# A reordered layer norm, more scan steps beside the first one, more buffers and doubled costs, in a two-layer image kernel

## The chip, the core and the metric

The kernel runs on one core of a Trainium2 chip. The core has five engines with instruction queues of their own: PE (TensorE, matrix products into PSUM), DVE (VectorE, elementwise work and scans), ACT (ScalarE, activation functions with a scale and a bias), POOL (GpSimd, elementwise work on SBUF) and SP (SyncE, which here only issues transfers). ACT and POOL issue transfers too. [...]PEld is the loading of weights into PE.

The metric is device time in microseconds (us) of one launch, the median of several runs.

## The reference

The input x is four images of 96 channels and 128 x 128 pixels, float32. Two residual layers follow each other, and only their skeleton matters here:

```python
# layer 0: a selective scan over the pixels in four orders
z  = silu(depthwise3x3(in_w @ groupnorm(x) + in_b))           # 192 channels
for k in range(4):                  # rows, columns, and both reversed
    delta, B, C = softplus(...), ..., ...                     # from z, per pixel
    h[t]  = exp(delta * A) * h[t-1] + delta * B * z[t]        # the scan
    ym   += C * h + D * z
yn = (ym - mean(ym)) * rsqrt(var(ym) + 1e-5)                  # over the 192 channels
x  = x + out_w @ (yn * ln_w + ln_b) + out_b                   # "the norm" below

# layer 1, on groupnorm(x)
xr, x1, x2 = relu_split_norm(groupnorm(x))    # positive and negative half, each normed
key, qry, value = conv3x3(x1), conv3x3(x2), conv3x3(x1)       # "the maps"
w  = softmax(unfold(key) @ unfold(qry).T)                     # 96 x 96 x 3 x 3 weights
y1 = layernorm(conv3x3(value, w))                             # "attention"
y2 = layernorm(conv3x3(x2, w_conv2)) * x1
x  = x + xr + w_full @ [y1, y2] + b_full
```

## The kernel before

The whole kernel is one launch. It is written as Python generators, one for each stage of each image. A generator emits a few instructions and then yields a number, its own estimate of what they cost. `co_run(left, right, pace)` runs two generators together: whenever `left` yields a cost, `right` is advanced until it has yielded `pace` times as much. So the numbers in the `yield` statements decide which instructions of two stages become neighbours in the engines' queues. `chain` puts generators one behind another, and `drain` runs one to its end.

The stages, in the order of the program:

1. `project` makes layer 0's inputs from each image; beside it runs `ssm_scan`, the scan over all four images. The scan advances in steps of 1024 pixels of 128 channels, each step in two half-steps that yield 2.6 each. A half-step issues three matrix products on PE (two of `pBC`, one of `pd`, line 736), and on DVE a product, the scan and a product (lines 826, 843, 847). A step has two operations on POOL (lines 822 and 855), and a softplus in two halves and an exponential on ACT (lines 665 and 798).
2. `norm` of image 0, then `split` of image 0, beside the scan at pace 0.5. `norm` is `ssm_output`, `split` is `split_norm`.
3. `direct_maps` of image 0, three convolutions done tap by tap (line 2102), beside the rest of the scan at pace 1.15; when the scan has ended, beside `norm` and then `split` of image 1 at pace 1.0. Only behind the scan, `lifting` is set: the value map is then read back, four rows at a time, turned into planes (`pixel_planes`, lines 1428 to 1437, on DVE) and stored for the last convolution. After each set of six rows up to four such lifts are made, and the rest at the end, by `lift(H)`.
4. `attend` of images 0 to 3, the `left` generator of the rest of the kernel. For image 0 only the last convolution remains (`direct_maps` made its maps). For the others it makes the maps in transformed planes (`products`, `outputs`, lines 1471 to 1564), the softmax, and the last convolution. Beside image b's attention runs what is called `light`: `norm` and `split` of image b+1 and `close` of image b-1 (`attn_output`, which makes the output rows of an image). Beside the last image there are no further `norm` and `split`; `light` is `close` of image 2 and then two passes of `LastOutput`: `before`, which prepares the last image's own x1 and residual, and `beside`, which can only start when the last image's maps are done.

The order in which the instructions were emitted is pinned, engine by engine, from the first projections to the end of the scan (`in_order(first)`). Behind that point a scheduler orders each engine's instructions, starting from the order of emission.

`ssm_output` works on 16 tiles of 1024 pixels in 18 passes of its loop; each pass handles three tiles: `new` (squares and sums), `mid` (variance, root, reciprocal) and `old` (output). For a `new` tile, ACT squares the 192 channels in two parts (`squares`, into the buffer `sq`, of which there is one), PE sums values and squares over the channels (`sums`, line 950), ACT copies the sums out and its queue sends them to 8 partitions (`rows`: `st`, `mq`). For `mid`, DVE makes the variance (`inverse`, lines 969 to 971), ACT its root (`roots`, line 975), DVE the reciprocal, and POOL's queue stores it to DRAM (`back`, line 988); `spread_out` reads it back, broadcast to 96 partitions, as `r` (line 996, POOL's queue), and `xr`, a tile of x from SP's queue, gets a bias on ACT. For `old`, PE projects the tile (`projected`, line 1002), DVE multiplies with `r` (line 1015, for image 0 line 1019), POOL adds `xr` (line 1016, for image 0 line 1020), DVE takes statistics (line 1021), and SP's queue stores the tile. In one pass these operations come in this order, with six yields between them:

```
projected(old, 0) | squares(new, 0) inverse(mid) roots(mid) scaled(old, 0) projected(old, 1) back(mid)
| sums(new, 0) squares(new, 1) bias and spread_out(mid) | scaled(old, 1) load_y sums(new, 1) | store(old) | rows(new) |
```

where `scaled` is the multiply, the add and the statistics in one.

`split_norm` reads the normed image twice. Its first pass only counts and sums (lines 1110 to 1117); its second pass makes the two halves x1 and x2. For image 0 each half of a tile is a buffer `half0` or `half1` (two of each) that POOL clears at its left edge, ACT scales, DVE thresholds (line 1230) and ACT's queue stores. For the other images the second pass also makes planes.

## Time and profile before

| | us |
|---|---|
| runs, median of 3 | 6656.29 |
| runs, lowest and highest | 6639.72, 6660.51 |
| profiled execution, its own time | 6633.8 |
| profiled execution, span of its instructions | 6631.9 |
| granted PE clock, mean over the span | 0.886 of full |

The profile belongs to one execution. Its own time lies below the lowest of the three runs, so a sum made from its durations is made against 6633.8 and then moved to the median. Durations, waits and stretches of time below are counted from the start of the span. A wait is listed as who waited, for whom, how long in total, how often, and the longest one. The stages begin as follows in it: the scan at 330, norm 0 at 2103, its split at 2384, the direct maps at 2545, the scan's end at 3290, image 0's last convolution at 3721, the maps of image 1 at 3867, of image 2 at 4730, of image 3 at 5775, and the last output at 6591.

### The profile page before, as it was taken

The numbers are of one execution on the slowest core, as the hardware profiler recorded it, in microseconds if no ns is written. First come the engines' busy times: TensorE is split into PE (matmuls) and PEld (weight loads), VectorE is DVE, ScalarE is ACT, GpSimd is POOL, SyncE is SP. The second block draws the span as 40 slices with busy tenths as digits, with TensorE's granted clock in tenths as the row PEclk, the third lists the DMA queues.
The fourth block names the chain that finished last, engine by engine and source line by source line (L and its number), as shares of the span: only waits on it lengthen the run. The fifth ranks groups of instructions, "written<-read, shape, count | busy, mean of one in ns | idle before, by whom it ended". The sixth has DMA issues, their size and how long they took to land. (4 is left out here: it accounts for less than half of the span.)

```text
span 6631.9 us, 76453 instructions
## 1 busy us (share of the span) xinstructions
PE 5374.8 (81%) x23264; PEld 2337.9 (35%) x23264; DVE 4907.7 (74%) x7469; ACT 3803.6 (57%) x4751; POOL 3506.9 (53%) x2744
## 2 busy tenths in 40 slices
PE   5889988987887736989987479877888777887988
PEld 2333323322222102444433134444333444344553
DVE  3247778988997568989755885588875788898666
ACT  1257768777786566676534464475544654545542
POOL 2236758978787436969621354466234574034320
PEclk9999989998997757999998789987988887998989
DMA  7766777866765667665666765655775555866547
GB/s 165 174 155 181 201 206 198 223 192 163 222 182 162 187 171 213 198 199 170 203 184 177 195 182 156 174 143 157 206 202 155 147 154 154 227 173 188 150 122 213
DMA packets 888487, 1198.29 MB, mean 181 GB/s; under 512 B 216143, under 2 KB 741015, under 8 KB 875597
## 3 DMA queue, kind: packets, MB, share of 16 engines
q1 hardware_dynamic: 864460, 1138.46, 63.1%
q0 software_dynamic: 16208, 38.42, 2.2%
q10 hardware_dynamic: 7408, 16.53, 0.8%
q8 instruction: 187, 3.06, 0.2%
q14 instruction: 224, 1.83, 0.1%
HBM read 777.62 MB, written 345.58 MB: 169 GB/s over the span
## 5 line engine op out<-in xcount | busy, mean ns | idle before, releaser
L622 PE MATMUL bank<-y,wp 128*128 128x512 f32 (+3 forms) x3584 | 1316.6, 624 | 85.5 <-DMA y<-y 34.4
L855 POOL TENSOR_TENSOR y<-y,dl 128x1024 f32<-128x1024 f32 x384 | 1056.4, 2751 | 272.1 <-DVE dl L847 238.0
L822 POOL TENSOR_TENSOR dl<-dl,u 128x1024 f32<-128x1024 f32 x384 | 1009.2, 2628 | 223.6 <-ACT dA L798 107.5
L843 DVE TENSOR_TENSOR_SCAN dA<-dA,pBC 128x512 f32<-128x512 f32 x768 | 981.5, 1278 | 30.7
L1471 PE MATMUL two<-ya,wd 128*64 128x192 f32 (+3 forms) x2376 | 595.1, 427 | 193.5 <-ACT odd L1542 96.8
L847 DVE TENSOR_TENSOR dl<-dA,pBC 128x512 f32<-128x512 f32 x768 | 528.0, 688 | 271.4 <-PE pBC L736 198.5
L736 PE MATMUL pBC<-xr,wbc 60*128 60x512 bf16 (+1 forms) x1536 | 458.8, 403 | 330.0 <-DVE dA L843 257.7
L622 PEld LDWEIGHTS bank<-y,wp 128*128 128x128 f32 (+3 forms) x3584 | 458.8, 169 | 754.2 <-issue 655.5
L2102 PE MATMUL bank<-y,wn 128*128 128x384 f32 (+5 forms) x2408 | 676.8, 504 | 43.0 <-DMA y<-x2d 18.9
L1905 ACT COPY yb<-ya 64x768 f32<-64x768 f32 (+1 forms) x660 | 537.8, 815 | 152.0 <-PE two L1471 111.7
L665 ACT ACTIVATE dl<-pd,dtb 128x512 f32<-128x512 f32 x768 | 485.6, 684 | 181.2 <-PE pd L736 171.3
L1471 PE MATMUL two<-yb,wd 128*64 128x192 f32 (+3 forms) x2376 | 567.6, 411 | 21.3 <-ACT yb L1905 21.3
L826 DVE TENSOR_TENSOR pBC<-dl,pBC 128x512 f32<-128x512 f32 x768 | 527.5, 687 | 9.7 <-POOL dl L822 8.8
L2102 PEld LDWEIGHTS bank<-y,wn 128*128 128x128 f32 (+3 forms) x2408 | 307.5, 167 | 338.9 <-issue 165.4
L798 ACT ACTIVATE dA<-dl,negA 128x1024 f32<-128x1024 f32 x384 | 420.3, 1141 | 2.3
L1471 PEld LDWEIGHTS two<-ya,wd 128*64 128x64 f32 (+1 forms) x2376 | 268.9, 172 | 405.4 <-ACT odd L1542 104.0
L736 PEld LDWEIGHTS <-wbc 60*128 60x128 bf16 (+1 forms) x1536 | 103.4, 96 | 767.7 <-issue 754.0
L665 ACT ACT_TABLE_LOAD x245 | 314.3, 1283 | 100.9 <-PE pd L736 93.6
L1975 POOL COPY own<-ring 32x512 f32<-32x512 f32 (+1 forms) x198 | 225.3, 1172 | 260.7 <-DVE ring L1564 224.4
L1471 PEld LDWEIGHTS two<-yb,wd 128*64 128x64 f32 (+1 forms) x2376 | 294.0, 173 | 167.5 <-issue 37.3
L2209 POOL MEMSET o<- 1x1024 f32 x60 | 56.3, 946 | 560.3 <-PE bank L2264 225.3
L1471 PE MATMUL two<-ya,wa 128*96 128x384 f32 (+1 forms) x528 | 230.1, 519 | 123.3 <-DMA ya<-vp 82.5
(323 smaller groups left out, 9936.6 us busy)
## 6 DMA issues: line engine op xcount, KB each, us to landing
u<-zb SPq DMA_DIRECT2D x192, 1024.0 KB
yms<-y SPq DMA_DIRECT2D x96, 512.0 KB
y<-yms SPq DMA_DIRECT2D x64, 768.0 KB
xn<-xnew SPq DMA_DIRECT2D x128, 384.0 KB
ya<-vp SPq DMA_DIRECT2D x120, 336.0 KB
y<-y SPq DMA_DIRECT2D x128, 258.2 KB
zb<-z SPq DMA_DIRECT2D x64, 512.0 KB
ya<-x1p SPq DMA_DIRECT2D x90, 336.0 KB
```

The lines of the kernel that those rows point to most:

```text
L622: nc.tensor.matmul(blocks(pz[p:e]), lhsT=ws[k][:, d, c : c + e - p], rhs=window(ys[k], at, d, n), start=(i == 0), stop=(i == len(terms) - 1),)
L665: nc.scalar.activation(dst, src, AF.Softplus, bias=bias)
L736: nc.tensor.matmul(p, lhsT=w[rows], rhs=xr[rows, at : at + CH], start=True, stop=True)
L798: nc.scalar.activation(live[m]["dA"], live[m]["dl"], AF.Exp, scale=negA[:, g % 3, k : k + 1])
L822: nc.gpsimd.tensor_mul(t, t, u_view(n))
L826: nc.vector.tensor_mul(p, live[n]["dl"][:, bass.ts(half, CH)], p)
L843: nc.vector.tensor_tensor_scan(h, h, p, init, ALU.mult, ALU.add)
L847: nc.vector.tensor_mul(live[n]["dl"][:, sl], live[n]["dA"][:, sl], live[n]["C", half])
L855: nc.gpsimd.tensor_add(v, v, t.rearrange("p (a b) -> p a b", b=W))
L1471: nc.tensor.matmul(of(to[p:e], r), lhsT=w[:, i, c : c + e - p], rhs=tiles(t[k][PAIR[i]][:, SLOT[i]], o, r), start=(k == 0), stop=False,)
L1905: nc.scalar.copy(yb[k][64 * h - 64 : 64 * h, :, :n], ya[k][0:64, :, h * TN : h * TN + n])
L2102: nc.tensor.matmul(pc[p:e, :n].rearrange("p (h w) -> p h w", w=W), lhsT=w[:, c : c + e - p], rhs=v[:, :, 0:W], start=(i == 0), stop=(i == ...
```

## The change

The change has four parts.

In `ssm_output`, `scaled` is taken apart into `scaled` (the multiply), `added` (the add) and `counted` (the statistics), and the operations of a pass are put in another order. `sq` gets two buffers, and the bank of PSUM for the sums is taken when the first sum is issued. With six yields of the same sizes as before, the pass becomes:

```
projected(old, 0) inverse(mid) squares(new, 0) | roots(mid) scaled(old, 0) projected(old, 1) squares(new, 1)
| back(mid) added(old, 0) scaled(old, 1) sums(new, 0) | sums(new, 1) added(old, 1) counted(old, 0) load_y
| rows(new) bias and spread_out(mid) counted(old, 1) | store(old) |
```

The pace of the scan beside norm 0 and split 0 goes from 0.5 to 0.65. The buffers `half0` and `half1` of image 0's split go from two to four each. And the costs yielded by `close` of image 2 and by `LastOutput.before` are doubled, so that they are spread over twice as much of the last image's attention.

The same operations are issued with the same shapes; nothing is added to or taken from the computation. The same line numbers hold up to line 940; behind it lines move by 3 to 17 (the sums are line 953 in the changed kernel, the multiplies 1015 and 1017, the statistics 1029).

```diff
--- before.py
+++ after.py
@@ -939,12 +939,15 @@
                     nc.sync.dma_start(ys[c], ym[:, :, bass.ts(c, SN)])
 
             def squares(c, j):
-                sq = p2.tile([C, SN], F32, name="sq", bufs=1)
+                sq = p2.tile([C, SN], F32, name="sq")
                 nc.scalar.activation(sq, ys[c][:, j], AF.Square)
-                sums_of[c] = sq, sums_of[c][1] if j else bank(ps)
+                sums_of[c, j] = sq
 
             def sums(c, j):
-                sq, pm = sums_of[c]
+                sq = sums_of.pop((c, j))
+                if j == 0:
+                    sums_of[c] = bank(ps)
+                pm = sums_of[c]
                 for g in range(4):
                     rhs = sq if g % 2 else ys[c][:, j]
                     nc.tensor.matmul(
@@ -954,12 +957,9 @@
                         start=(j == 0),
                         stop=(j == 1),
                     )
-                if j == 0:
-                    squares(c, 1)
-
             def rows(c):
                 st = p2.tile([128, CH], F32, name="st", bufs=1)
-                nc.scalar.copy(st, sums_of.pop(c)[1])
+                nc.scalar.copy(st, sums_of.pop(c))
                 mq = made[c] = p2.tile([RS, 2, W], F32, name="mq")
                 for i in range(2):
                     nc.scalar.dma_start(mq[:, i], st[32 * i : 32 * i + 65 : 64])
@@ -1009,16 +1009,24 @@
                 return po
 
             def scaled(c, h, po):
+                r = near[c][1][:, bass.ts(h, CH)]
+                if turned:
+                    v = r.rearrange("p (h j t) -> p h j t", t=TN, j=TW)
+                    nc.vector.tensor_mul(v, turned_view(po), v)
+                else:
+                    nc.vector.tensor_mul(r, po, r)
+
+            def added(c, h):
                 xr, r = (t[:, bass.ts(h, CH)] for t in near[c])
                 if turned:
                     v = r.rearrange("p (h j t) -> p h j t", t=TN, j=TW)
-                    nc.vector.tensor_mul(v, turned_view(po), v)
                     nc.gpsimd.tensor_add(v, v, turned_view(xr))
-                    xr = r
                 else:
-                    nc.vector.tensor_mul(r, po, r)
                     nc.gpsimd.tensor_add(xr, r, xr)
-                nc.vector.bn_stats(stats[:, 2 * c + h], xr)
+
+            def counted(c, h):
+                t = near[c][turned]
+                nc.vector.bn_stats(stats[:, 2 * c + h], t[:, bass.ts(h, CH)])
 
             for c in range(3):
                 load_y(c)
@@ -1028,37 +1036,46 @@
                 mid = c - 1 if 1 <= c <= NS else None
                 if old is not None:
                     po = projected(old, 0)
-                yield 1.2
+                if mid is not None:
+                    inverse(mid)
                 if new:
                     squares(c, 0)
+                yield 1.2
                 if mid is not None:
-                    inverse(mid)
                     roots(mid)
                 if old is not None:
                     scaled(old, 0, po)
                     po = projected(old, 1)
                     ys.pop(old)
+                if new:
+                    squares(c, 1)
+                yield 1.4
                 if mid is not None:
                     back(mid)
+                if old is not None:
+                    added(old, 0)
+                    scaled(old, 1, po)
+                if new:
+                    sums(c, 0)
                 yield 1.4
                 if new:
-                    sums(c, 0)
+                    sums(c, 1)
+                if old is not None:
+                    added(old, 1)
+                    counted(old, 0)
+                    load_y(c + 1)
+                yield 1.4
+                if new:
+                    rows(c)
                 if mid is not None:
                     xr = near[mid][0]
                     nc.scalar.activation(xr, xr, AF.Identity, bias=outbs)
                     spread_out(mid)
-                yield 1.4
                 if old is not None:
-                    scaled(old, 1, po)
-                    load_y(c + 1)
-                if new:
-                    sums(c, 1)
+                    counted(old, 1)
                 yield 1.4
                 if old is not None:
                     nc.sync.dma_start(xnew[:, bass.ts(old, SN)], near.pop(old)[turned])
-                yield 1.4
-                if new:
-                    rows(c)
                 yield 1.4
 
     def split_norm(xnew, x1d, x2d, stats, keep, cnt, ps, side, planes, vector, done):
@@ -1215,7 +1232,7 @@
                         )
                         k, parts = TW * R, 2
                     else:
-                        h = p2.tile([C, RS * PW], F32, name=f"half{side_}")
+                        h = p2.tile([C, RS * PW], F32, name=f"half{side_}", bufs=4)
                         hv = h.rearrange("p (h w) -> p h w", w=PW)
                         nc.gpsimd.memset(hv[:, :, 0:1], 0.0)
                         v, to = y.rearrange("p (h w) -> p h w", w=W), hv[:, :, 1:PW]
@@ -2227,7 +2244,7 @@
     def plain(v):
         return v.rearrange("p (h t j) -> p h t j", j=TW, t=TN)
 
-    def attn_output(img, ps, side):
+    def attn_output(img, ps, side, share):
         ob = out[img.b].rearrange("c h w -> c (h w)")
         with (
             tc.tile_pool(name="f1", bufs=1, side=side) as p1,
@@ -2267,7 +2284,7 @@
                         nc.vector.tensor_add(x1[:, sl], pf, e[:, sl])
                     else:
                         nc.vector.tensor_add(plain(x1[:, sl]), pixels(pf), pixels(e[:, sl]))
-                    yield 2.6
+                    yield 2.6 * share
                 nc.sync.dma_start(ob[:, bass.ts(t, SN)], x1)
 
     class LastOutput:
@@ -2303,9 +2320,9 @@
                         ahead = load(t + 1)
                     x1, e = (p3.tile([C, SN], F32, name=n) for n in ("x1", "e"))
                     first_half(img, xx, x1)
-                    yield 2.0
+                    yield 4.0
                     residual(img, xx, e)
-                    yield 2.6
+                    yield 5.2
                     for d, y in ((self.x1d, x1), (self.ed, e)):
                         nc.sync.dma_start(d[:, bass.ts(t, SN)], y)
 
@@ -2418,10 +2435,10 @@
         def attend(self, at):
             yield from attention(self, at)
 
-        def close(self, ps, side):
+        def close(self, ps, side, share=1.0):
             while not self.finished:
                 at.later.tick()
-            yield from attn_output(self, ps, side)
+            yield from attn_output(self, ps, side, share)
 
     npair = NB // 2
     zb, yms = (
@@ -2482,7 +2499,7 @@
     imgs = {0: Image(0)}
     imgs[0].begin()
     left = chain(imgs[0].norm(yms[0][0], psl, "left"), imgs[0].split(psl, "left"))
-    co_run(left, last, 0.5)
+    co_run(left, last, 0.65)
     drain(left)
     left = direct_maps(imgs[0], psl)
     co_run(left, last, 1.15)
@@ -2536,7 +2553,7 @@
                 after.append(
                     imgs[b + 1].split(psr, "right", lambda i, second: second)
                 )
-            after.append(imgs[b - 1].close(psr, "right"))
+            after.append(imgs[b - 1].close(psr, "right", 1.0 if b + 1 < NB else 2.0))
             if b + 1 == NB:
                 last = imgs[b].last = LastOutput(imgs[b], psr, "right")
                 imgs[b].maps_made = lambda: maps_made(last)
```

## The prediction

> **What bounds the kernel now.** I read the page first, then busy time by stretch, cut where the program changes stage, then the waits inside each stretch. The page says that no engine is full over the whole span:
>
> ```profile
> PE 5374.8 (81%) x23264; PEld 2337.9 (35%) x23264; DVE 4907.7 (74%) x7469; ACT 3803.6 (57%) x4751; POOL 3506.9 (53%) x2744
> ```
>
> So the stages have to be priced one by one. In the answer by stretch the columns are the stretch, its length, then busy us of PE, PEld, DVE, ACT, POOL, the granted PE clock, the DMA share and GB/s:
>
> ```profile
> 2103.00:2384.00 281.00, 188.02 (x476) 44.02 (x475) 146.81 (x223) 146.63 (x162) 130.18 (x96) 0.67 0.65 183
> 2384.00:2545.00 161.00, 30.62 (x61) 7.34 (x62) 125.04 (x172) 120.04 (x147) 41.18 (x47) 0.50 0.67 196
> 2545.00:3290.00 745.00, 686.76 (x2911) 319.25 (x2910) 644.78 (x784) 506.75 (x639) 630.27 (x239) 0.97 0.67 194
> 3290.00:3639.00 349.00, 286.77 (x1100) 122.97 (x1098) 175.43 (x473) 132.36 (x207) 72.63 (x135) 0.91 0.68 181
> 3639.00:3721.00 82.00, 0.25 (x2) 0.00 (x0) 81.66 (x224) 19.25 (x26) 31.71 (x62) 0.50 0.61 162
> 3721.00:3950.00 229.00, 182.59 (x775) 85.78 (x776) 199.15 (x332) 150.70 (x198) 107.64 (x134) 0.91 0.76 206
> 5810.00:6150.00 340.00, 273.46 (x1408) 141.98 (x1408) 295.67 (x377) 162.91 (x186) 135.33 (x137) 0.89 0.65 181
> 6150.00:6400.00 250.00, 231.74 (x1734) 155.30 (x1734) 151.72 (x294) 127.54 (x172) 111.70 (x166) 0.97 0.48 126
> ```
>
> In order: norm 0 beside the scan; split 0 beside the scan; image 0's direct maps beside the scan; the same beside norm 1; a gap of 82 us in which PE does nothing while VectorE is full; image 0's last convolution; and two halves of the last image's maps. Norm 0 has nothing full: it is a chain of waits. The waits in 2103 to 2384 us (total, times, longest) show its links:
>
> ```profile
> DVE xstats L1021 <- POOL xr L1020: 95.6, 32, 9.0
> POOL r L996 <- DMA rd<-mq: 49.0, 12, 6.9
> ACT mq L975 <- DVE mq L971: 46.7, 14, 6.6
> PE bank L950 <- ACT sq L943: 31.3, 15, 7.6
> ```
>
> Each is an operation emitted straight behind its producer, with scan steps queued behind it. The gap is one wait; in norm 2 (4019 to 4300 us) PE waits for the two things that norms 1 and 3 show too:
>
> ```profile
> PE two L1471 <- DMA ya<-vp: 82.5, 1, 82.5
> ...
> PE bank L950 <- DVE r L1015: 14.4, 6, 5.3
> PE bank L950 <- ACT sq L943: 7.5, 10, 4.2
> ```
>
> **What the Trainium skill says.** "TensorE: Matmul & The Clock Gate", Part 1: PE runs at half clock unless recently kept busy. The trace agrees: 0.50 where PE works 31 of 161 us, 0.97 at 687 of 745. So part of norm 0's 188 us of PE is slow clock, which denser work would shorten. The same page, "Architectural detail", calls VectorE and ScalarE strict FIFO: the 95.6 us in front of the statistics hold scans too. "DMA: Bandwidth & Descriptors", "Rules for kernel authors": issue a transfer early and wait late. Here r's broadcast lands in 3.5 us (median) in norm 0 and 4.9 in norm 2, with up to 9.6.
>
> **The change, part by part.** I used the built programs' instruction order for what moves; durations are the trace's.
>
> **A, norm 0.** Nothing is computed less. Statistics move a step behind the add, the add behind the multiply, the second Square to its own buffer, the root behind the variance, the broadcast's issue (POOL queue) two steps behind the reciprocal's store, the xr load's use two steps behind its SP issue. Up to its last statistics the norm now emits 31 scan half-steps instead of 24. Seven more cost VectorE 7 x (1.278+0.688+0.687) = 18.6 us, so 165 us. ACT: 146.6, plus 32 mq issues of 0.52 = 163; then 10 softplus halves of 0.68, 4 exponentials of 1.14, 5 copies of 1.14 and some 5 table loads of 1.28, 24 us: 187. PE: 188 at clock 0.67, plus 21 matmuls of 0.4 = 196, less if the clock rises. Floors of 165 to 196 stand against 281; the 95.6 us of statistics waits alone are a third. I take back a third of the 85 us of slack: **-28**. Ends: -55 if the waits vanish, +10 if the new steps only add work (18.6 us of VectorE, half hidden). What is late next is the variance (L969), which waits for mq's DMA behind ScalarE's copy and issues, and ScalarE itself; scans stand behind L969 on VectorE.
>
> **B, split 0.** 23 half-steps instead of 18. Its first pass is full on ScalarE (42.6 of 43 us, 2398 to 2441), so two there cost some 2 x 2 us; the other three fall in the second pass, VectorE 79 of 93 us, 3 x 2.65 = 8 more, within 93. Four buffers remove waits for the halves' stores: ScalarE 20.9+9.1 us and POOL's memsets 41.0+20.1, all inside those 93 us, of which VectorE already covers 79. Net **+2**, ends -12 and +12.
>
> **C, direct maps beside the scan.** 14 half-steps leave this stage. PE is at 92%, so PE prices them: a scan matmul takes (458.8+209.8)/2304 = 0.29 us, 14 x 3 x 0.29 = **-12**. At POOL's price, (2.75+2.63)/2 each, 38; at least 0, as they return in A and B. One set of 56 direct matmul instructions of 1204 passes behind the scan's end; that is a move, not a saving.
>
> **D, the gap.** Image 0's value map is lifted into planes (L1428 to L1437, 124.4 us over 32 lifts, 3.89 each) only after the scan, four lifts a set. Behind the softmax's last scaling (L1694) stand 12 lifts, 12 thresholded halves of image 1 (0.74) and some 2.5 plane sets (6.9): 73 us of VectorE, which is the gap; SP's queue holds the first ya loads behind those lifts' stores. With one set more behind the scan and the light work further on, the changed order has 5 lifts, 4 halves and under one set there: 28 us. The moved work goes beside the direct maps, where VectorE is busy 175 of 349 us. Loading the made weights stays. **-42**, ends -15 (weights or stores then wait) and -50.
>
> **E, norms 1 to 3.** PE stood before the sums (L950) for r 38.4 us and for sq some 21 us in all, 60 us. But r's broadcast now has 4.0 pace units before its multiply, not 6.8; a norm of 149.6 units takes about 277 us, so 7.4 us instead of 12.6 against a landing of about 5. I take a quarter of the 60: **-14**. Ends -60 and +60.
>
> **F, image 0's convolution.** At the lifts' end 20 halves are done instead of 12, so two tiles of some 10 us VectorE leave a stage where VectorE is busy 199 of 229 and PE 183. Three tenths counts: **-6**, ends -20 and 0.
>
> **G, last image.** Doubled costs spread image 2's output and image 3's first pass over combining groups 122 to 155 of image 3's maps (softmax at 164) instead of 122 to 140. Over 5810 to 6400 PE is busy 505 of 590 us, VectorE 447. At the second half's 92.7% PE the same work takes 545, -45; three quarters of the stretch is reached, and VectorE would be at 80%: **-30**. Ends -60 and +10 (a wait for the combining now met everywhere). SP's and POOL's issues only move.
>
> Sum: -28 + 2 - 12 - 42 - 14 - 6 - 30 = **-130**. The profiled execution took 6633.8 us (span 6631.9 and 1.9 around it), giving 6504. The runs' median, 6656.3, is 22 above it, so **6526**.
>
> **Rivals.** One: **the waits only change name.** Norm 0 stays at 281 us with its extra scans, E and G give nothing: 2 - 12 - 42 - 6 = -58, 6598. For: ScalarE and half-clock PE would fill 190 us there. Against: 95.6 us of waits on an add of 1.27 us. Two: **the scheduler undoes it.** Order is pinned only up to the scan's end; behind it a scheduler orders norms 1 to 3, and in its order the statistics still stand next to the multiplies. Then E is 0: 6540, inside the forecast. Three: **more than the sum**, PE's clock rises in norm 0 and C goes at POOL's price: -55 - 38 in place of -28 - 12, G -45: -198, 6458. Four, **slower: r late on VectorE.** If each of 64 tiles waits x us more for r at L1015/L1019, with scans and attention's combining queued behind and PE behind those, 64x stands against 116 (the sum without E). It decides from x = 2.1 us; at 2.5 the result is +44, 6700. For: VectorE already waits 80.0 us for r in norms 1 to 3, 1.7 a tile. Against: PE saw only 38.4 of that.
>
> **Numbers.** Forecast 0.62 (with rival two), waits renamed 0.20, more 0.10, slower 0.08. About 0.3%, 20 us, can be told from no change. Some of the second case ends within it: faster 0.85, same 0.07, slower 0.08. The range leaves out the slower case, the no-change part and a few of the largest gains: 6445 to 6625.
>
> **What would show it.** A: norm 0 with split 0 under 430 us, statistics waits under 30 us. C, D: PE idle behind the direct maps about 40 us, not 82. E: waits at the sums (L953 after) under 45 us. G: the last maps shorter, VectorE even over them. Wrong if the gap stays above 70 us, if waits for r exceed 200 us, or if norm 0 is not shorter.

## The result, and the profile after

The changed kernel takes 6566.19 us (median of 6 runs, 6550.88 to 6586.09); the kernel before took 6648.84 us beside it (6 runs). The ratio is 0.9876, interval [0.9854, 0.9898]: 83 us less, where the forecast was 130. The profiled execution's own time is 6572.02 us, its span 6570.2. Between the two spans lie 61.7 us, fewer than between the medians, because the profiled execution of before (6633.8) lies 15 us below its median and that of the changed kernel 6 us above.

The page's busy line hardly differs from the one before:

```profile
PE 5365.0 (82%) x23264; PEld 2348.1 (36%) x23264; DVE 4934.7 (75%) x7469; ACT 3806.4 (58%) x4757; POOL 3533.2 (54%) x2744
```

Busy time by stretch, cut at the same stages (stretch, length, busy us of PE, PEld, DVE, ACT, POOL, clock, DMA share, GB/s). The last three lines are the last image's maps, whole and in halves:

```profile
2103.00:2373.00 270.00, 195.88 (x502) 46.67 (x500) 187.19 (x249) 172.85 (x189) 147.95 (x104) 0.64 0.73 206
2373.00:2539.00 166.00, 38.68 (x76) 9.11 (x77) 140.02 (x186) 130.67 (x157) 61.60 (x53) 0.50 0.64 194
2539.00:3236.00 697.00, 644.16 (x2743) 298.93 (x2743) 608.78 (x739) 472.78 (x599) 595.67 (x225) 0.97 0.66 196
3236.00:3650.00 414.00, 323.96 (x1218) 142.57 (x1216) 232.33 (x598) 152.95 (x240) 113.16 (x184) 0.87 0.67 174
3650.00:3698.00 48.00, 1.64 (x9) 1.35 (x9) 43.74 (x127) 6.93 (x10) 22.72 (x32) 0.50 0.72 192
3698.00:3848.00 150.00, 125.59 (x394) 51.00 (x396) 128.29 (x209) 105.00 (x138) 59.77 (x75) 0.92 0.85 232
...
5726.00:6348.00 622.00, 541.83 (x3278) 318.72 (x3278) 480.97 (x711) 311.45 (x382) 255.66 (x305) 0.91 0.59 161
...
5726.00:6037.00 311.00, 274.19 (x1408) 143.31 (x1409) 255.81 (x353) 139.59 (x167) 111.31 (x125) 0.91 0.60 163
6037.00:6348.00 311.00, 267.64 (x1871) 175.41 (x1869) 225.16 (x359) 171.85 (x215) 144.35 (x180) 0.90 0.58 160
```

Three stretches are shorter (norm 0, the direct maps beside the scan, the gap) and one is much longer: the direct maps behind the scan, 414 us instead of 349, with VectorE busy 232 us in it instead of 175.

The waits in norm 0 (who waited, for whom, total, times, longest):

```profile
POOL rd L988 <- DVE mq L986: 90.5, 15, 8.9
...
PE bank L953 <- ACT sq L943: 30.3, 10, 5.8
DVE xstats L1029 <- POOL xr L1025: 26.7, 18, 1.9
DVE r L1017 <- DMA r<-rd: 21.9, 11, 4.0
...
ACT mq L975 <- DVE mq L971: 12.2, 6, 5.3
POOL r L996 <- DMA rd<-mq: 11.6, 5, 5.2
```

The statistics' 95.6 us became 26.7, the root's 46.7 became 12.2 and the broadcast's 49.0 became 11.6. New at the top is POOL before the reciprocal's store, 90.5 us; in the kernel before it was

```profile
POOL rd L988 <- DVE mq L986: 27.9, 15, 1.9
```

PE's wait for the Squares stayed (31.3, now 30.3). PE's waits from the scan's end to image 0's last convolution:

```profile
PE two L1488 <- DVE half L1247: 41.2, 1, 41.2
PE bank L2119 <- DMA y<-x2d: 22.5, 5, 8.4
PE bank L1720 <- DVE sm L1711: 18.6, 1, 18.6
PE bank L2119 <- DMA y<-x1d: 17.7, 4, 13.6
```

The gap is half of its 82.5 us. But the direct maps now wait for their own input tiles (y, 40.2 us), and the step with the softmax's result (L1720) waits for VectorE. In the kernel before, the same waits were

```profile
PE bank L2102 <- DMA y<-x2d: 13.7, 4, 5.5
PE bank L1703 <- DVE sm L1694: 5.4, 1, 5.4
PE bank L2102 <- DMA y<-x1d: 0.7, 2, 0.5
```

The length of each stage, taken from the first and last instructions of the lines that bound it, shows the whole ledger. The program is the same up to the scan's end in the changed kernel and in four of the runs below (split held, no r, no r with its broadcast, last image). In these five profiles norm 0 took 258.9 to 264.2 us and the direct maps beside the scan 672.4 to 681.4, so differences under some 5 us, in the long stages under some 9, are not read.

| stage, us | before | after | order alone | pace alone | after, pace 0.5 | after, split held |
|---|---|---|---|---|---|---|
| norm 0 | 274.7 | 264.2 | 242.8 | 300.5 | 243.8 | 258.9 |
| split 0 | 171.8 | 176.7 | 172.2 | 183.8 | 166.1 | 176.7 |
| direct maps beside the scan | 726.0 | 678.5 | 724.3 | 676.6 | 725.7 | 681.3 |
| behind the scan, to the softmax | 352.0 | 418.6 | 353.6 | 425.4 | 344.1 | 362.8 |
| gap | 86.3 | 49.5 | 86.5 | 49.4 | 86.5 | 26.6 |
| image 0's last convolution | 145.5 | 150.4 | 148.8 | 147.6 | 159.4 | 184.1 |
| maps of image 1 | 726.1 | 717.4 | 720.7 | 722.9 | 723.2 | 724.0 |
| its last convolution | 136.3 | 158.2 | 135.3 | 158.9 | 138.5 | 139.0 |
| maps of image 2 | 847.2 | 800.6 | 854.3 | 810.9 | 842.3 | 886.0 |
| its last convolution | 198.0 | 201.4 | 201.1 | 201.5 | 197.4 | 197.2 |
| maps of image 3 | 628.5 | 622.0 | 629.1 | 628.5 | 618.7 | 618.7 |
| the rest | 228.5 | 222.2 | 228.0 | 225.7 | 228.3 | 222.2 |

### The profile page after: what moved, and what is told of

It reads as the page before. It is cut to its first block, busy times and chain, and to the rows that moved or that the text cites. A ratio compares the mean times of both kernels' runs of the same rounds, so it can differ in the third digit from the quotient of the medians.

```text
span 6570.2 us, 76328 instructions
## 1 busy us (share of the span) xinstructions
PE 5365.0 (82%) x23264; PEld 2348.1 (36%) x23264; DVE 4934.7 (75%) x7469; ACT 3806.4 (58%) x4757; POOL 3533.2 (54%) x2744
## 5 line engine op out<-in xcount | busy, mean ns | idle before, releaser
L622 PE MATMUL bank<-y,wp 128*128 128x512 f32 (+3 forms) x3584 | 1317.3, 626 | 86.3 <-DMA y<-y 33.8
L1002 PE MATMUL bank<-y,outws 96*96 96x512 f32 x512 | 298.3, 717 | 5.5 <-DVE r L1017 2.7
```

Source lines behind the costliest of these rows:

```text
L622: nc.tensor.matmul(blocks(pz[p:e]), lhsT=ws[k][:, d, c : c + e - p], rhs=window(ys[k], at, d, n), start=(i == 0), stop=(i == len(terms) - 1),)
```

## The experiments

### The four parts, each alone

To the kernel before: the norm's new order with its second `sq`; the pace; the doubled costs; the four buffers.

```diff
 p1_order: the change's edits of ssm_output, with
-                sq = p2.tile([C, SN], F32, name="sq", bufs=1)
+                sq = p2.tile([C, SN], F32, name="sq")
 p2_pace:
-    co_run(left, last, 0.5)
+    co_run(left, last, 0.65)
 p3_costs: the change's edits of attn_output, close, the call of close, and LastOutput.before, with
-                    yield 2.6
+                    yield 2.6 * share
 p4_bufs:
-                        h = p2.tile([C, RS * PW], F32, name=f"half{side_}")
+                        h = p2.tile([C, RS * PW], F32, name=f"half{side_}", bufs=4)
```

> The norm's new order and second sq buffer alone; pace 0.5, two half buffers, costs of the last image as before. Theory A (the parts add up; what is missing against the forecast was lost where the pace part moves work to the end of image 0's direct maps): norm 0 some 15 us shorter than 281, norms 2 and 3 with what surrounds them some 20 shorter, the gap before image 0's convolution unchanged at 82: -25 to -45 us in all. Theory B (the order only pays together with the higher pace, because it makes room for scan steps): norm 0 over 275 us, total -15 us or less.

> Pace 0.5 to 0.65 beside norm 0 and split 0 alone. Theory A: norm 0 and split 0 longer by some 15 us for 12 to 14 more half-steps, the direct maps beside the scan shorter by 45, the end of the direct maps longer by 60, the gap shorter by 35: -5 to -30 in all. Theory B: norm 0 is a chain of waits that the added steps lengthen at their full VectorE price, 12 x 2.65 = 32 us, and the total is between -5 and +20.

> Doubled costs of the last image's light work alone. The changed kernel's maps of image 3 were 6 us shorter in its profile, so theory A: -3 to -12 us, VectorE even over these maps, PE idle about 80 of 622 us as there. Theory B (the forecast's -30 was right and other parts of the change took it back): -20 us or more.

> Four buffers for image 0's halves alone. Theory A: the second pass of split 0 stays at about 93 us, because VectorE is full there: 0, between -6 and +4. Theory B: ScalarE's 30 us and POOL's 61 us of waits for stores set that pass's length: -15 us.

| alone | median, us | ratio to before | interval | of 6650 us |
|---|---|---|---|---|
| order | 6604.7 | 0.9921 | [0.9907, 0.9936] | -52 |
| pace | 6647.08 | 1.0 | [0.9989, 1.0011] | 0 |
| costs | 6638.25 | 0.9984 | [0.9972, 0.9996] | -11 |
| buffers | 6645.28 | 0.999 | [0.9982, 0.9998] | -7 |

The parts sum to -70 us, against -83 with an interval of some 15 to either side: no interaction is needed to explain the total. The order gave more than either of its theories allowed; the pace came out as its theory B has the total, the costs as their theory A, and the buffers 1 us beyond their theory A. Most of the gain is the order's; its second `sq` buffer was not tried apart from it. The pace, which carried C and D of the prediction, is worth nothing.

Norm 0 with the order alone, its split, and the direct maps behind the scan, by stretch:

```profile
2107.00:2350.00 243.00, 174.49 (x476) 42.93 (x477) 155.86 (x224) 144.77 (x161) 124.45 (x93) 0.73 0.72 205
2350.00:2522.00 172.00, 30.97 (x61) 6.96 (x60) 128.88 (x169) 127.76 (x153) 51.31 (x55) 0.50 0.67 195
3246.00:3592.00 346.00, 294.63 (x1111) 127.42 (x1110) 167.16 (x436) 125.79 (x198) 71.40 (x130) 0.87 0.68 179
```

The statistics' wait in norm 0, 95.6 us before, is with the order alone

```profile
DVE xstats L1029 <- POOL xr L1025: 29.6, 23, 1.9
```

The order takes 32 us from norm 0, and leaves the other stages where they were, within the spread named above. The ratio gives -52, 20 us more. Between the two profiled executions lie only 28, as that of before lies 16 us below the median of its runs here; the other 20 us stand in no stage that these traces tell apart.

### Other paces

To the changed kernel: `co_run(left, last, 0.5)`, and 0.8.

> The changed kernel with the old pace of 0.5 beside norm 0 and split 0: what the higher pace is worth once the norm has its new order. Theory A (the seven steps cost norm 0 and split 0 some 25 us and give back some 45 behind it, new order or not): 15 to 25 us above the changed kernel, 6581 to 6592. Theory B (with the new order the steps find room, and the pace is worth the forecast's 60): above 6605. Theory C (it is worth nothing, as it was with the old order): within 8 us of the changed kernel.

> The changed kernel with pace 0.8. Another 14 half-steps go ahead of the direct maps. Theory A: norm 0 and split 0 longer by some 25 to 30 us, the direct maps beside the scan shorter by 46 and one more set behind the scan, +40 to +60; the gap of 48 us can shrink by 15 at most, as only 5 lifts are left in it: -5 to +20 against the changed kernel. Theory B: again -20 or more.

Pace 0.5: 6559.84 us, ratio to before 0.9879 [0.9862, 0.9896], the same as with 0.65, as theory C has it. Pace 0.8: 6610.85 us, 0.9952 [0.9938, 0.9966], which gives back over half of the gain and lies outside both theories. The scans in norm 0 say what a half-step costs. The columns are the operation and its count, the lowest, mean and highest ns, and when they ran. First the kernel before (pace 0.5, norm 0 of 274.7 us):

```profile
L843 DVE TENSOR_TENSOR_SCAN dA<-dA,pBC x27: 1221/1279/1280, 2116.0 to 2374.8; 128x512 f32<-128x512 f32 x27
```

In the changed kernel:

```profile
L843 DVE TENSOR_TENSOR_SCAN dA<-dA,pBC x36: 1221/1279/1281, 2109.5 to 2366.3; 128x512 f32<-128x512 f32 x36
```

One of the 36 began 1 us before the norm did, so eight more start within it. With the new order, norm 0 takes 243 to 244 us with 27 scans (order alone; pace 0.5), 259 to 264 with 35 (the five profiles named above) and 286 with 44 (pace 0.8): 15 to 21 us for eight, 42 for seventeen, or 2.3 to 2.5 us each on average. With the old order eight cost 300.5 - 274.7 = 26 us, 3.2 each. A half-step's three VectorE operations take 1.278 + 0.688 + 0.687 = 2.65 us. So a half-step put beside norm 0 costs about its whole VectorE time, although VectorE is busy only 156 of 243 us there. That VectorE is the engine on which it is paid is not shown: from the order alone to the five profiles VectorE's busy time in norm 0 grows by some 25 us, but ScalarE's by 27.5 and PE's by 17 to 23. The prediction's A had priced the steps far lower.

### Image 1's split held back

To the changed kernel: image 1's split is not started before the direct maps are done.

```diff
-    light = chain(
-        imgs[1].norm(yms[0][1], psr, "right"),
-        imgs[1].split(psr, "right", lambda i, second: second),
-    )
+    light = imgs[1].norm(yms[0][1], psr, "right")
     co_run(left, light, 1.0)
     drain(left)
+    light = chain(light, imgs[1].split(psr, "right", lambda i, second: second))
```

> The changed kernel, in which image 1's split is held back until image 0's direct maps are done; only norm 1 runs beside them. Theory T1 (the set that moved behind the scan took 58 us there and not 36 because the split, pulled forward with it, fills VectorE at the end of the direct maps and holds up their loads and the softmax): from the scan's end to the end of the direct maps 375 to 385 us instead of 404, the softmax right behind. Theory T2 (a set simply costs some 60 us beside a norm, because PE is shared): 395 us or more. In total +-15 for both, since the split then lies beside image 0's convolution, where VectorE is at 86%.

6580.99 us, 0.9912 [0.9897, 0.9926]. From the scan's end to the end of the direct maps:

```profile
3218.50:3566.50 348.00, 317.64 (x1238) 139.68 (x1235) 168.05 (x469) 93.86 (x145) 77.23 (x145) 0.92 0.66 175
```

With the set of maps that moved into it and none of the split, that stage takes 348 us; with the split it takes 404 (both without the 15 us to the softmax). The stage of before, 344, had a set less and a part of the split. In the last 50 us of it the changed kernel's VectorE is the full engine, and PE is not:

```profile
3586.00:3636.00 50.00, 32.48 (x126) 20.00 (x126) 48.33 (x113) 19.97 (x34) 25.89 (x37) 0.76 0.57 146
```

So the split's share of the changed stage costs 56 us there, although VectorE is busy only 232 of 414 us over the whole stage. Theory T1 is right, by more than it said: PE's waits for the direct maps' own tiles, 40.2 us in the changed kernel, are 1.3 us with the split held back. But held back it costs as much and more later: image 0's convolution +34 us, the maps of image 2 +85, against -56 behind the scan, -23 in the gap and -19 in image 1's convolution. The ratios put the change of this one edit at +0.36 points, 24 us, with intervals that just touch; T1 had allowed 15.

### What waiting for r costs in norms 1 to 3

Three edits of the changed kernel: no r at all in norms 1 to 3 (the multiply takes a constant tile); the same with the broadcast still read, into a spare DRAM tensor; and the broadcast issued one step earlier.

```diff
 q4_no_r:
-                nc.gpsimd.dma_start(r, to.partition_broadcast(C))
+                if not turned:
+                    nc.gpsimd.dma_start(r, to.partition_broadcast(C))
-                    nc.vector.tensor_mul(v, turned_view(po), v)
+                    nc.vector.tensor_mul(v, turned_view(po), w)   # w: a constant
 s2_traffic: as q4_no_r, and
+                if turned:
+                    nc.gpsimd.dma_start(spare, to.partition_broadcast(C))
 s1_spread_earlier:
                     nc.scalar.activation(xr, xr, AF.Identity, bias=outbs)
-                    spread_out(mid)
...
                     sums(c, 1)
+                if mid is not None:
+                    spread_out(mid)
                 if old is not None:
                     added(old, 1)
```

> The changed kernel without r in norms 1 to 3: r is not read back from DRAM and the projection is multiplied by a constant, so these three norms leave their inverse deviation out. It shows what the waits for r and the transfers are worth there. Theory A (PE is the bound beside these norms and the waits for r only move its idle time): stretches of norms 1 to 3 each within 8 us, total -5 to -20. Theory B (the 30 us of PE waits behind r at the sums, and VectorE's 50 us, are lost time that a better order would win): -30 to -60.

> As the run without r (the projections of norms 1 to 3 multiplied by a constant, their inverse deviation left out), but the broadcast of 384 KB is still issued from POOL's queue, into a spare tensor in DRAM that nobody reads. Theory A (what the run without r won is the wait for r): again 50 to 75 us below the changed kernel. Theory B (it is the transfer's share of the queues and of POOL's queue): within 20 us of the changed kernel.

> The changed kernel with the broadcast of r issued one step earlier (1.4 pace units behind the reciprocal's store instead of 2.8), so 5.4 units ahead of its multiply instead of 4.0. If the lead of r is what PE loses in norms 1 to 3 (theory A), the waits of L1015 for r fall from 50 us to 30 or less and the total by 10 to 25 us. If the scheduler places these operations by its own estimates whatever the order of emission (theory B), the waits stay at 40 us or more and the total within 8 us. Norm 0, where the order is pinned, shows it either way: its 22 us of waits for r go, and POOL waits longer for the store (12 us now, up to 40).

| | median, us | ratio to before | interval | against after |
|---|---|---|---|---|
| no r | 6497.29 | 0.9784 | [0.9771, 0.9797] | -61 us |
| no r, broadcast kept | 6532.26 | 0.9843 | [0.9829, 0.9856] | -22 us |
| broadcast a step earlier | 6556.96 | 0.9882 | [0.9867, 0.9898] | same |

(The last column is the difference of the ratios, by 6650 us.) So in norms 1 to 3 some 60 us hang on r, as theory B of the first run has it. With the broadcast kept only 22 of them are won, between the two theories of the second run. By the intervals of the two ratios it can be 5 to 39 us; by the three stages of these norms it is 29 of 60. So a third to a half is the wait for the value, and the rest goes with the transfer and what it holds up. One such thing shows in the groups: VectorE's wait for POOL's add, first without the broadcast and then with it.

```profile
L1034 DVE BATCH_NORM_STATS2 xstats<-r 96x6 f32<-96x512 f32 x96 | 65.3, 683 | 102.6 <-POOL r L1028 102.3
L1037 DVE BATCH_NORM_STATS2 xstats<-r 96x6 f32<-96x512 f32 x96 | 65.3, 683 | 152.2 <-POOL r L1031 152.0
```

The kept broadcast goes to DRAM and not to SBUF; what that changes was not tried. Issuing the broadcast a step earlier buys nothing. Theory B of that run holds, the wait for r staying over 40 us:

```profile
L1015 DVE TENSOR_TENSOR r<-bank,r 96x512 f32<-96x512 f32 x96 | 63.6, 673 | 86.6 <-DMA r<-rd 43.2 <-issue 15.1 <-PE bank L1002 13.0
```

In norm 0, where the order is pinned, the wait for r does go (21.9 to 0.5 us), and POOL's wait for the store's landing (11.6 to 37.4) and the statistics' wait (26.7 to 53.9) grow instead. The groups of the changed kernel show where the norms stand (line, operation, count | busy, mean ns | idle time before it, by releaser):

```profile
L953 PE MATMUL bank<-y,mean 96*32 96x512 f32 x512 | 206.8, 733 | 48.9 <-DVE r L1015 30.0 <-DMA y<-yms 15.9 <-issue 2.9
L953 PE MATMUL bank<-sq,mean 96*32 96x512 f32 x512 | 164.6, 750 | 39.7 <-ACT sq L943 39.6
L1029 DVE BATCH_NORM_STATS2 xstats<-r 96x6 f32<-96x512 f32 x96 | 66.0, 687 | 124.8 <-POOL r L1023 124.6
L1015 DVE TENSOR_TENSOR r<-bank,r 96x512 f32<-96x512 f32 x96 | 63.7, 674 | 86.5 <-DMA r<-rd 49.7 <-PE bank L1002 16.3 <-issue 10.5
```

And in the kernel before:

```profile
L950 PE MATMUL bank<-y,mean 96*32 96x512 f32 x512 | 239.4, 720 | 58.0 <-DVE r L1015 38.4 <-DMA y<-yms 13.9 <-ACT st L962 5.6
L950 PE MATMUL bank<-sq,mean 96*32 96x512 f32 x512 | 166.2, 730 | 52.6 <-ACT sq L943 52.6
L1021 DVE BATCH_NORM_STATS2 xstats<-r 96x6 f32<-96x512 f32 x96 | 65.9, 686 | 104.3 <-POOL r L1016 104.0
L1015 DVE TENSOR_TENSOR r<-bank,r 96x512 f32<-96x512 f32 x96 | 63.5, 674 | 129.3 <-DMA r<-rd 80.0 <-PE bank L1002 24.5 <-issue 14.1
```

VectorE's wait for r fell from 80.0 to 49.7 us, while its wait for the add rose from 104.0 to 124.6.

### The two transfers on another queue

To the changed kernel: the reciprocal's store and the broadcast go through SP's queue.

```diff
-                nc.gpsimd.dma_start(to.rearrange("(p f) -> p f", f=W), q)
+                nc.sync.dma_start(to.rearrange("(p f) -> p f", f=W), q)
-                nc.gpsimd.dma_start(r, to.partition_broadcast(C))
+                nc.sync.dma_start(r, to.partition_broadcast(C))
```

> The changed kernel with the two transfers around r (the store of the reciprocal and the broadcast that reads it back) issued by SP's queue instead of POOL's; nothing else differs. In the changed kernel POOL stands before the store for 90.5 us in norm 0 and 85.3 us in norms 1 to 3, with its adds queued behind, and VectorE's statistics then wait 130 us for those adds. Theory A, POOL's queue is where the norms lose time: statistics waits fall by half or more, norm 0 falls from 264 to some 245 us and the three norm stages by some 5 us each, total 6566 - 20 - 15 = about 6530. Theory B, the wait only moves: SP then stands before the store with the loads of ym, x and the combining's planes queued behind, PE and ScalarE wait for loads, norm 0 stays at 264 or grows and the total lies between 6560 and 6610.

6538.39 us (4 runs), 0.9856 [0.9838, 0.9875]; span 6525.4. Its groups:

```profile
L1023 POOL TENSOR_TENSOR r<-r,xr 96x512 f32<-96x512 f32 x96 | 145.6, 1535 | 307.8 <-DVE r L1015 243.5 <-ACT sq L943 23.3 <-DMA rd<-mq 21.9
...
L1029 DVE BATCH_NORM_STATS2 xstats<-r 96x6 f32<-96x512 f32 x96 | 66.2, 690 | 127.9 <-POOL r L1023 127.7
L1015 DVE TENSOR_TENSOR r<-bank,r 96x512 f32<-96x512 f32 x96 | 60.8, 670 | 26.7 <-DMA r<-rd 14.9 <-PE bank L2119 11.5
...
L1029 DVE BATCH_NORM_STATS2 xstats<-xr 96x6 f32<-96x512 f32 x32 | 21.2, 678 | 1.9 <-POOL xr L1025 1.8
```

And SP's own waits, among others:

```profile
SPq L988 <- DVE mq L986: 117.7, 16, 13.2
...
SPq L988 <- DVE mq L981: 90.5, 24, 7.8
```

In the changed kernel POOL's wait there is, for norms 1 to 3,

```profile
POOL rd L988 <- DVE mq L981: 146.1, 32, 15.2
```

and not the 85.3 us of the expectation. Each theory holds in one place. In norm 0, whose order is pinned, B is right on the length: the statistics wait only 1.9 us instead of 26.7, but SP stands before the store for 117.7 us instead of POOL's 90.5, and norm 0 takes 275.0 us instead of 264.2. Behind the scan, A's total is nearly met and its reason is not: the stages of norms 1 to 3 take 404.6, 698.1 and 782.6 us instead of 418.6, 717.4 and 800.6 (image 1's convolution takes 14 us more), while the statistics wait as long as before (127.7); what fell is the wait for r, 49.7 to 14.9. Whether the broadcast lands sooner from SP's queue is not shown, as the trace has no time to landing for it. The profiled spans differ by 45 us, the ratios by 0.2 points, 13 us, with intervals that overlap, so this version is faster than the kernel before, and perhaps faster than the changed one. "DMA: Bandwidth & Descriptors", "Issuing engines are not separate DMA queues", says that another issuing engine saves only the time to issue. On POOL that time is in the trace, 128 issues at 0.53 us, 68 us; the run does not separate it from the time that POOL stood before them.

### The last image without part of its VectorE work

To the changed kernel: `LastOutput.before` makes each of its two tiles with one ScalarE operation.

```diff
-                    first_half(img, xx, x1)
+                    nc.scalar.activation(x1, xx, AF.Identity, scale=scale[:, 0:1], bias=shift[:, 0:1])
                     yield 4.0
-                    residual(img, xx, e)
+                    nc.scalar.activation(e, xx, AF.Identity, scale=up[:, 0:1], bias=up[:, 1:2])
                     yield 5.2
```

> The changed kernel without the three VectorE operations of each tile in the last image's first pass (its x1 and residual are then ScalarE's output alone, so thresholds and the residual's last term are left out there): 16 x (1.32+1.39+1.36) = 65 us of VectorE fewer under image 3's maps. Theory A (VectorE work there costs PE time at nearly its own length wherever it is put, since the combining of PE's results stands behind it; so spreading it could win little): -35 to -60 us. Theory B (spread out, it is hidden, and PE is the bound; the forecast failed because PE was not idle for that reason): 0 to -15 us.

6522.87 us, 0.9836 [0.9819, 0.9852], 27 us under the changed kernel by the ratios. The last image's maps by stretch:

```profile
5703.00:6295.00 592.00, 524.02 (x3278) 311.34 (x3278) 413.68 (x663) 311.40 (x384) 233.89 (x305) 0.93 0.61 170
```

67 us of VectorE less (481.0 to 413.7) made the stage 30 us shorter (622 to 592), although VectorE was busy 77% of it and evenly so. This lies between the two theories: spread out as it is, the work is not free and costs nearly half its length. What it would save where it stood before was not tried. The path is open too: POOL's busy time in the stage fell by 22 us (255.7 to 233.9) for the same 305 instructions.

## Why the prediction was right, and where it was wrong

Faster was right, and the range holds the result. The mechanism held for the order in norm 0 and for the gap; A, E, F and G were mis-sized, and between C and D the price of the moved work was left out. That the range holds the result is in part luck: C and D, 54 of the 130 us, paid nothing once all stages are counted, and the order paid 52 by its run where A and E together had 42. Measured terms are stage lengths of the two profiled executions, so they stand against their 61.7 us; where a run measured a part alone, it is named.

**A, norm 0: forecast -28, measured -10.5.** Two parts against each other. The order alone gives -32 and takes most of the statistics' waits with it; the prediction's own rule, a third of the slack, gives 31 without the extra steps (281 - 188 = 93), but that third was assumed, so the agreement is partly luck. The step that failed is the price of the extra steps. In the forecast they only raise the floor from 188 to 196 us, which costs the term 3 us, and even its bad end has "18.6 us of VectorE, half hidden". They came to eight half-steps and cost 15 to 21 us, 2.3 each. What was named as late next, the variance behind mq's transfer, was not (7.9 us at L969). POOL's 90.5 us before the store are the longest wait, but with the store on SP's queue norm 0 was not shorter. "TensorE: Matmul & The Clock Gate", Part 1, was cited for a clock that denser work would raise. With the order alone it did rise, from 0.67 to 0.73; with the extra steps it lay at 0.63 to 0.68 in the five profiles, about where it was before.

**B, split 0: forecast +2, measured +5.** Buffers -6 (165.6 and 166.1 with four at pace 0.5, 170.7 to 172.2 with two), pace +11 to +12.

**C and D, the direct maps and the gap: forecast -54, measured -18.** D is right: 49.5 us of gap instead of 86.3, -37 where -42 was forecast; 7 lifts and 8 halves stand in it, where 5 and 4 had been counted. C's first half fits: -47.5 us beside the scan, which is the 12 of the forecast if the one set that moved behind it takes some 35; the two were not measured apart. The step that failed is the sentence "the moved work goes beside the direct maps, where VectorE is busy 175 of 349 us". That stage grew by 66.6 us. About 35 of it would then be the set; the rest is light work of image 1 that came forward, and the split held back prices its share at 56. The half-idle VectorE was no cover: it filled at the stage's end (48.3 of 50 us), and PE stood 40.2 us before the direct maps' tiles, 1.3 with the split held back. The average over the stage hid that.

The pace as a whole thus nets to nothing: +31 us in norm 0 and its split, -47 beside the scan, +75 behind it, -37 in the gap, and -36 in the later stages (the maps of image 2 are 42 us shorter, 842.3 to 800.6, and image 1's convolution 20 longer; all as differences of after and after at pace 0.5). With the order of before they are +38, -49, +73, -37 and -14. The sums, -14 and +11, lie to both sides of the 0 that the runs give.

**E, norms 1 to 3: forecast -14, measured nothing that can be told from 0.** With the order alone the three stages take 353.6, 720.7 and 854.3 us against 352.0, 726.1 and 847.2. Rival two was right: the scheduler leaves the statistics about as close to their multiplies as they were. From a multiply to its own statistics it is 3.3 places in VectorE's order in norms 1 to 3 before, 3.8 with the order alone and 3.9 in the changed kernel; in norm 0, where the order is pinned, it was 1 place in all 32 cases and became 2 to 6. The mark set for E was met all the same: in the whole span PE stood 30.0 us before the sums for r and 39.6 for sq, 30.3 of these in norm 0, so 39 us in norms 1 to 3 instead of 60. With the order alone it is 44.5, and the three stages together are no shorter: a wait that falls is not time won. The 33 us that the changed kernel saves in the maps of images 1 and 2 and the convolution between (-8.7 + 21.9 - 46.6) do not appear with the order alone; with the pace alone part of them does (-3.2 + 22.6 - 36.3), and held back the split makes image 2's maps 85 us longer. At pace 0.5, with the rest of the change in place, 6 of the 33 are left. So they go with the pace and the split pulled forward, and not with the order.

**F, image 0's convolution: forecast -6, measured +5.** 25 halves are done when it begins instead of 17, as many more as forecast. But 32 are made within it, where 30 were, and VectorE is busy 128.7 us in it instead of 125.3: later light work took their place. The pace alone shows the same, 25 and 30 halves and 147.6 us.

**G, the last image: forecast -30, measured -11 by the costs alone.** In the two profiles the maps are 6.5 us shorter and what follows them 6.3. VectorE became as even as was said: 255.8 and 225.2 us in the two halves, 281.7 and 196.1 before:

```profile
5775.00:6089.00 314.00, 261.44 (x1272) 130.32 (x1272) 281.65 (x364) 147.49 (x170) 114.70 (x113) 0.91 0.65 178
6089.00:6403.00 314.00, 273.37 (x2006) 180.53 (x2006) 196.11 (x348) 164.30 (x213) 134.70 (x192) 0.93 0.52 141
```

PE did not fill: busy 541.8 of 622 us, 87%, where 92.7% had been taken from the quiet stretch. The step that failed is to carry that share over: in the quiet stretch VectorE was busy 152 of 250 us, and spreading the work leaves no stretch as quiet. That the light work is what keeps PE below it is in part shown: without some of it the maps are 30 us shorter.

**The marks set beforehand:** norm 0 with its split under 430 us: 436 in the stretches shown, missed; statistics' waits under 30: 26.7, met; the gap about 40: 48, nearly; waits at the sums under 45: 39, met without a gain; the last maps shorter: by 6.5 us. Of the three signs of being wrong none came: the gap is not above 70, VectorE's waits for r are 71.6 us in all, and norm 0 is shorter.

## What to carry to other kernels

Put each consumer one step behind its producer where queues are strict and the order is pinned; it was the one part of four that paid much, 0.8%. Price work that is moved beside other work at what it costs there when added and taken away, not at zero because the engine's average is at half: here it cost some 2.3 of 2.65 us in a stage at 64% VectorE, and nearly half in one at 77%. And make the ledger over all later stages: a gap half closed here was paid for in the stage ahead of it.

## What the runs showed of the hardware

A broadcast can cost more than the wait for its value. That of r is 384 KB and lands in 5.3 us (median over the changed kernel, from issue to landing). Some 60 us hang on 48 of them in norms 1 to 3; of these, 22 by the runs or 29 by the stages are the wait for the value, and the rest goes with the transfer.

The clock of PE in norm 0 did not follow the amount of work alone. The same 476 matmuls ran at 0.67 in 275 us and, in the new order, at 0.73 in 243 us; with 500 matmuls in 259 to 264 us it was 0.63 to 0.68, though at 1.9 per us they came nearly as densely as the 1.96 of the new order alone. What lowers it there stays open.
